# A graph layer on one core: reordering stores, loads, POOL sums and copies around two node loops

## The chip, the cores and the metric

The kernel runs on one core of one Trainium2 chip. The metric is the device time of one launch in microseconds (us); the time before is the median of three runs. The profile is that of one further execution on the hardware.

The core's engines are named as the profile names them: PE is TensorE (its matmuls; PEld are its weight loads), DVE is VectorE, ACT is ScalarE, POOL is GpSimd, SP is SyncE, which here only issues DMA transfers. "SPq" in the profile is SyncE's queue. Each engine runs its own instructions in the order in which the program lists them.

## The reference, cut to what matters

There are 32 graphs of 512 nodes with 256 features each. For each graph:

```python
h = jnp.maximum(_layernorm(x), 0.0)
# branch 1: two convolutions along the node axis
h1 = relu(bn1(conv1(h)))              # 1 tap
x_conv = relu(bn2(conv2(h1)) + h)     # 17 taps
# branch 2: messages over the graph
s = h @ w_se.T + b_se                 # 3 numbers a node
A = jnp.exp(-dist(s)) * adj           # 512 x 512
msg = relu(h @ w_msg.T + b_msg)
x_nmp = jnp.einsum('bnm,bmd->bnd', A, msg)
# a GRU cell of [x_conv, x_nmp] and h
out = x + gru(concat([x_conv, x_nmp]), h)
```

All arithmetic is in float32.

## The kernel before, in words

The graphs are worked through in two groups of 16 (`GB = 16`, `NG = 2`), and then in 16 pairs. The program is written out by hand: inside `tc.manual_schedule()` each engine's instructions stand in the order in which the Python code emits them.

**First part** (`first_part`, one call for each group). For each graph b: load x (`load_x`), layer norm (`statistics`: DVE bn_stats and bn_aggr, then POOL's power for rstd; `normalise`: on DVE, or on ACT with a DVE-made shift), transpose to features by nodes (`transpose_h`, with a store of h to DRAM, HD), the one-tap convolution (`conv1`), and a Fourier transform of windows of 64 nodes (`windows_to_freq`), which is how the 17-tap convolution is computed: it becomes a product per frequency. `between` and `left` bring other work in between: in group 0 the weights' transform, in group 1 the last four products of group 0 (units 36 to 39, run by `fill`) and the gates' weights.

**Node loop** (`nodes`, one call for each group). It walks over the 16 graphs of the group (`todo`) and at the same time over 40 frequencies ("units"). For a unit u, `product` multiplies the group's spectra by the weights in three products (the third with sums: `prepare` has POOL make `wsum` from the loaded weights and `both` from the spectra), and ACT and DVE combine them into y, which is stored to DRAM (YD). Weights come by `load_unit`, 512 KB each, into three buffers; `multiply(u)` first flushes pending stores, runs the product, prepares unit u + 2 and loads the next weights.

For a graph, `message` makes msg and s; `features`, `factors`, `exponents` make exp(-dist) in four tiles; `turn` transposes the loaded adjacency (`load_adj`, 1 MB in four transfers) on DVE, and `masked` multiplies it in, also on DVE; the aggregation is either `aggregate7`, with seven block products in place of eight and eight sums by POOL ahead of it (`block_sums`, `message_sums`, `affinity_sums`), or the plain `aggregate`. Both write a tile `nmp` (one buffer), which is stored to DRAM (ND) by `save_nmp`. `load_h` brings h back from DRAM, and `by_chunks` copies it on ACT into a tile with the tag `hq` (two buffers), which `message` of the same graph reads later.

One iteration i of the loop thus emits, in this order: the loads of adj for the graph after next and of h for the fourth next; the stores that are pending (y of the last unit, nmp of the graph before); factors of the next graph; the first product; the message of the graph after next; half of the mask of the next graph; the second product; the other half; the aggregation of graph b; the h copy; the block sums of the next graph; the third product, if there is one. Group 0 has 36 units for 16 graphs, so two products in most iterations and three in four of them; group 1 has 40 units for its first 13 graphs, three in nearly all. In group 1 the last two graphs use the plain aggregation, since there the next stage begins to use POOL.

**The pairs** (from line 1164): gates of the GRU by products with combined weights (`inverse`, `gates_rz`, `gate_n`), 16 pairs long, from about 860 us to the end.

**What sets the order around the change.** All transfers of the node loops leave one queue, SyncE's. A transfer that has to wait (a store for the engine that makes its data, a load for the readers of the buffer that it overwrites) holds up all behind it in that queue. Likewise on POOL, `wsum` waits for the weights' transfer and for the product that read the buffer before, and everything behind it waits too. The pools named "first", "sums", "seven", "nodes" share memory one after the other: a tile of a later stage waits for the readers of what lay there before.

Of the kernel before, what the change touches and what calls it, by code (L numbers as in the profile page):

```python
# [11 lines left out]
FP = mybir.dt.float32  # L12
# [3 lines left out]
P = 128  # L16
# [49 lines left out]
def gnn_layer(  # L66
# [16 lines left out]
    B, N, D = x.shape  # L83
# [3 lines left out]
    DC = D // P  # L87
# [28 lines left out]
    def load_x(b, queue=nc.sync):  # L116
        X[b] = pools["ahead" if b == GB else "first"].tile([P, NC, D], FP, tag="x", name=f"x_{b}", bufs=1 if b == GB else 3)
        queue.dma_start(X[b], x[b].rearrange("(c p) d -> p c d", p=P))
# [186 lines left out]
    def transpose_h(b):  # L305
# [9 lines left out]
        nc.sync.dma_start(HD[b], HT[b])  # L315
        del XN[b]

    def conv1(b):
        H1[b] = pools["first"].tile([P, NC, D], FP, tag="h1", name=f"h1_{b}", bufs=2)
        h = N // D  # L320
        for c0 in range(0, NC, h):
            p = bank(f"pc1_{b}_{c0}").rearrange("p (c d) -> p c d", d=D)
            for j in range(h):
                c = c0 + j
                for ic in range(DC):
                    nc.tensor.matmul(p[:, j, :], HT[b][:, ic, c * P : (c + 1) * P], w1[:, ic, :],  # L326
                                     start=(ic == 0), stop=(ic == DC - 1))
            h1 = H1[b][:, c0 : c0 + h, :]
            nc.vector.tensor_add(h1, p, shift1_row[:, None, :].to_broadcast([P, h, D]))
            nc.scalar.activation(h1, h1, AF.Relu)  # L330
        if b % GB < GB - 2:
            del HT[b]
# [90 lines left out]
    def by_chunks(b):  # L423
        HQ[b] = work.tile([P, DC, N], FP, tag="hq", name=f"hq_{b}", bufs=2)
        for ic in range(DC):
            nc.scalar.copy(chunks(HQ[b][:, ic, :]), by_chunk(HT[b][:, ic, :]))
        del HT[b]
# [89 lines left out]

    def aggregate(b, dcs=range(2)):
        if 0 in dcs:
            NMP[b] = work.tile([P, DC, N], FP, tag="nmp", name=f"nmp_{b}", bufs=1)  # L520
        for dc in dcs:
            p = bank(f"pn_{b}_{dc}")
            for mc in range(NC):
                nc.tensor.matmul(p, MSG[b][:, mc, dc * P : (dc + 1) * P], A[b][:, mc, :],
                                 start=(mc == 0), stop=(mc == NC - 1))
            nc.scalar.copy(NMP[b][:, dc, :], p)
        if DC - 1 in dcs:
            del MSG[b], A[b]
# [353 lines left out]
    def first_part(g, freq, between, left=()):  # L882


        b0, b1 = g * GB, (g + 1) * GB
        for b in range(b0, b0 + 3):
            if b not in X and (g == 0 or b == b0):
                load_x(b)
        if g == 0:
            t = XN[b0] = pools["first"].tile([P, NC, D], FP, tag="xn", name="rows", bufs=2)  # L890
            ones, diags = t[:, 0, :P], t[:, 1:3, :].rearrange("p i (c m) -> p i c m", m=P)
            nc.vector.memset(ones, 1.0)

            for _ in range(5):
                nc.tensor.matmul(row1[1][:, : 2 * P], ident, fr.rearrange("p c g k -> p (c g k)")[:, : 2 * P], start=True, stop=True)
            batch_norm("bn1", scale1, shift1, nc.gpsimd)
            bn1_row(0, scale1, ones, diags)
            bn1_row(1, shift1, ones, diags)
        if b0 not in STATS:
            statistics(b0)  # L900
        normalise(b0)
        if g == 0:
            scale_w1()
            shift_w1()
        left = list(left)

        def fill():
            for step in left.pop(0) if left else ():
                step()

        if g > 0:
            load_x(b0 + 1)
            fill()
            load_x(b0 + 2)
        transpose_h(b0)
        fill()
        statistics(b0 + 1)
        if g > 0:
            statistics(b0 + 2)
        normalise(b0 + 1, g > 0)  # L920
        fill()
        for b in range(b0, b1):
            if b + 3 < b1:
                load_x(b + 3, nc.sync if b < 3 else nc.gpsimd)
            if b == b0:
                conv1(b)
                one, two = between(0) if g == 0 else ([], [])
                for step in one:
                    step()
                fill()  # L930
                if g == 0:
                    transpose_h(b + 1)
                    statistics(b + 2)
                    normalise(b + 2)
                else:
                    normalise(b + 2)
                    transpose_h(b + 1)
                fill()
                xf, last_two = freq(g), two
                continue  # L940
            if g == 0:

                slots = last_two if b == b0 + 1 else between(b - b0)

                def slot():
                    for step in slots.pop(0) if slots else ():
                        step()

                if b == b0 + 1:
                    between(b - b0)  # L950
                    conv1(b)
                    slot()
                if b == b0 + 2:
                    slot()
                if b == b1 - 1:
                    by_chunks(b - 1)
                    load_h(b0)
                if b + 2 < b1:
                    statistics(b + 2)
                if b + 1 < b1:  # L960
                    transpose_h(b + 1)
                if b > b0 + 2:
                    slot()
                if b + 2 < b1:
                    normalise(b + 2)
                if b > b0 + 1:
                    conv1(b)
                    slot()
                if b == b1 - 1:
                    by_chunks(b)  # L970
                windows_to_freq(b - 1, xf)
                slot()
                continue
            if b + 2 < b1:
                statistics(b + 2)
            if b + 1 < b1:
                transpose_h(b + 1)
            if b + 2 < b1:
                normalise(b + 2)
            one, two = between(b - b0)  # L980
            conv1(b)
            if b == b1 - 1:
                by_chunks(b - 1)
                load_h(b0)
            for step in one:
                step()
            windows_to_freq(b - 1, xf)
            for step in two:
                step()
        if g > 0:  # L990
            by_chunks(b1 - 1)
        windows_to_freq(b1 - 1, xf)
        return xf
# [8 lines left out]
    with tc.tile_pool(name="freq", bufs=1) as fpool:  # L1002
# [33 lines left out]
        def nodes(g, xf, units, last, following=()):  # L1036
# [45 lines left out]
            for i, b in enumerate(todo):  # L1082
                mine = spread(units, i, last) if i < last else []
                more = todo[i + 1 : i + 5]
                seven = i <= last

                def bring():
                    if len(more) > 1:
                        message(more[1])
                        features(more[1])  # L1090

                if g + 1 < NG and i == GB // 2:
                    load_x(b1)
                if g + 1 < NG and i == 3 * GB // 4:
                    statistics(b1)
                if len(more) > 1:
                    load_adj(more[1], i % 2)
                if len(more) > 3:
                    load_h(more[3])
                flush()  # L1100
                if more:
                    factors(more[0])
                if i == 0:
                    bring()
                for u in mine[:1]:
                    multiply(u)
                if i > 0:
                    bring()
                if not seven:
                    aggregate(b, [0])  # L1110
                if more:
                    turn(more[0], [0, 1])
                    exponents(more[0])
                    masked(more[0], [0, 1])
                for u in mine[1:2]:
                    multiply(u)
                if more:
                    turn(more[0], [2, 3])
                    masked(more[0], [2, 3])
                if seven:  # L1120
                    aggregate7(b)
                else:
                    aggregate(b, [1])
                if len(more) > 2:
                    by_chunks(more[2])
                stores.append(partial(save_nmp, b))
                if more and i + 1 <= last:
                    block_sums(more[0])
                for u in mine[2:]:
                    multiply(u)  # L1130
            flush()

        with phase("pw", "ahead"):
# [103 lines left out]
```

## Time and profile before

| what | us |
|---|---|
| median of three runs | 1827.38 |
| lowest, highest | 1824.57, 1829.56 |
| span of the profiled execution | 1824.8 |
| first part, group 0 | 0 to about 152 |
| node loop, group 0 | about 152 to 445 |
| first part, group 1 | about 445 to 565 |
| node loop, group 1 | about 565 to 860 |
| gates of the 16 pairs | about 860 to 1825 |

The stages are read off the timeline by the lines that run. The profile has several views. The page gives busy time by engine and the chain of work that ended last: followed back from the last instruction, each step names what released it. The view of waits lists, for an engine and a line, how long it stood idle and whose instruction ended the wait, as total, number of times and longest. The view of stretches gives busy time in windows. The timeline lists instructions with start, length, engine, source line, output and inputs, and in brackets how long the engine was idle before it, and because of whom. Matmuls are pipelined, and their ends in the profile are modelled, so a stall of TensorE is best measured from start to start.

### The profile page before, as it was taken

The numbers are of one execution on the slowest core, as the hardware profiler recorded it, in microseconds if no ns is written. First come the engines' busy times: TensorE is split into PE (matmuls) and PEld (weight loads), VectorE is DVE, ScalarE is ACT, GpSimd is POOL, SyncE is SP. The second block draws the span as 40 slices with busy tenths as digits, with TensorE's granted clock in tenths as the row PEclk, the third lists the DMA queues.
The fourth block names the chain that finished last, engine by engine and source line by source line (L and its number), as shares of the span: only waits on it lengthen the run. The fifth ranks groups of instructions, "written<-read, shape, count | busy, mean of one in ns | idle before, by whom it ended". The sixth has DMA issues, their size and how long they took to land.

```text
span 1824.8 us, 21188 instructions
## 1 busy us (share of the span) xinstructions
PE 1796.3 (98%) x6974; PEld 1152.3 (63%) x6974; DVE 1244.0 (68%) x2370; ACT 623.0 (34%) x1252; POOL 779.1 (43%) x731
## 2 busy tenths in 40 slices
PE   9999999999999999999999999999999999999998
PEld 6777788788897887886545554555445554555444
DVE  7886889896995787686266556664666456655666
ACT  4556444442345444443212221222222221222121
POOL 3432868777333777776421332223231323133221
PEclk9999999999999999999999999999999999999999
DMA  9999977975668887888242244214422443234412
GB/s 259 310 292 227 248 215 209 240 216 180 232 222 214 232 239 211 228 226 282 68 118 69 56 121 121 87 35 121 121 89 36 118 121 104 50 89 121 116 22 53
DMA packets 307089, 288.27 MB, mean 158 GB/s; under 512 B 146764, under 2 KB 237420, under 8 KB 306596
## 3 DMA queue, kind: packets, MB, share of 16 engines
q1 hardware_dynamic: 296948, 261.44, 53.3%
q0 software_dynamic: 6592, 23.50, 4.1%
q10 hardware_dynamic: 3440, 1.97, 0.4%
q8 instruction: 56, 0.92, 0.2%
q14 instruction: 53, 0.43, 0.1%
HBM read 190.45 MB, written 96.40 MB: 157 GB/s over the span
## 4 chain that ended last, share of the span: by engine, by line
PE 84%; DMA 5%; DVE 4%; POOL 2%; issue 2%; SPq 1%; ACT 1%; ACTq 0%; DVEq 0%; POOLq 0%
PE pg L667 30%; PE pn L667 15%; PE py L390 8%; PE pn L541 8%; PE pc L326 5%; PE pc L655 5%; PE pm L441 4%; PE px L341 3%; DMA wt<-wd 2%; PE pw L254 2%; PE phT L310 1%; PE pd L485 1%; DMA nd<-nmp 1%; PE pz L667 1%; DVE A L491 1%
## 5 line engine op out<-in xcount | busy, mean ns | idle before, releaser
L645 POOL TENSOR_TENSOR hp<-hp 128x512 f32<-128x512 f32 x64 | 80.4, 1267 | 413.9 <-DMA hp<-hd 294.6
L667 PE MATMUL pg<-hp,sw 128*128 128x512 f32 x434 | 222.0, 593 | 0.7 <-DVE rz L686 0.5
L667 PE MATMUL pg<-cp,sw 128*128 128x512 f32 x434 | 221.8, 593 | 0.0
L667 PE MATMUL pg<-np,sw 128*128 128x512 f32 x434 | 221.7, 592 | 0.0
L645 POOL TENSOR_TENSOR cp<-cp 128x512 f32<-128x512 f32 x64 | 80.5, 1267 | 231.8 <-ACT cp L661 230.5
L390 PE MATMUL py<-wt,xf 128*128 128x256 f32 x640 | 156.3, 388 | 0.2 <-DVE y L398 0.2
L682 ACT ACTIVATE rz<-rz,brz 128x512 f32<-128x512 f32 x93 | 67.0, 722 | 260.2 <-DVE rz L686 260.2
L357 POOL TENSOR_TENSOR wsum<-wt 128x512 f32<-128x512 f32 x78 | 102.9, 1319 | 111.0 <-DMA wt<-wd 90.4
L667 PEld LDWEIGHTS pg<-hp,sw 128*128 128x128 f32 x434 | 82.3, 190 | 104.6 <-issue 96.7
L667 PEld LDWEIGHTS pg<-np,sw 128*128 128x128 f32 x434 | 82.6, 190 | 103.7 <-issue 103.7
L667 PEld LDWEIGHTS pg<-cp,sw 128*128 128x128 f32 x434 | 82.6, 190 | 103.7 <-issue 103.7
L390 PEld LDWEIGHTS py<-wt,xf 128*128 128x128 f32 x640 | 118.2, 192 | 35.5 <-issue 20.5
L806 ACT ACTIVATE nt<-nt,vech 128x512 f32<-128x512 f32 x64 | 46.2, 722 | 236.2 <-DVE nt L805 236.2
L441 PE MATMUL pm<-wmsg,hq 128*128 128x259 f32 x512 | 118.5, 383 | 1.0 <-DVE nmp L559 1.0
L326 PE MATMUL pc<-w,hT 128*128 128x256 f32 x512 | 117.9, 383 | 0.8 <-DVE hT L314 0.8
L491 DVE TENSOR_TENSOR A<-A,at 128x512 f32<-128x512 f32 x128 | 113.6, 925 | 6.0 <-ACT A L487 6.0
L667 PE MATMUL pn<-np,sw 128*128 128x512 f32 x224 | 114.5, 593 | 0.0
L667 PE MATMUL pn<-hp,sw 128*128 128x512 f32 x224 | 114.5, 593 | 0.0
L667 PE MATMUL pn<-cp,sw 128*128 128x512 f32 x224 | 114.5, 593 | 0.0
L326 PEld LDWEIGHTS pc<-w,hT 128*128 128x128 f32 x512 | 94.8, 190 | 23.9 <-issue 5.6
L441 PEld LDWEIGHTS pm<-wmsg,hq 128*128 128x128 f32 x512 | 96.2, 190 | 17.2 <-DVE nmp L559 2.5
L655 PEld LDWEIGHTS pc<-back,yt 128*128 128x128 f32 x640 | 92.7, 190 | 7.6 <-issue 7.6
(173 smaller groups left out, 3429.1 us busy)
## 6 DMA issues: line engine op xcount, KB each, us to landing
wt<-wd SPq DMA_DIRECT2D x80, 512.0 KB, 6.9
adj<-in_adj_dram SPq DMA_DIRECT2D x128, 256.0 KB, 7.6
wd<-wst SPq DMA_DIRECT2D x64, 320.0 KB, 5.9
yd<-y SPq DMA_DIRECT2D x76, 256.0 KB, 7.5
yt<-yd SPq DMA_DIRECT2D x30, 640.0 KB, 6.7
hd<-hT SPq DMA_DIRECT2D x32, 512.0 KB, 5.3
nd<-nmp SPq DMA_DIRECT2D x32, 512.0 KB, 4.2
xb<-in_x_dram SPq DMA_DIRECT2D x128, 128.0 KB, 3.7
```

The costliest lines, as they stand in the source:

```text
L326: nc.tensor.matmul(p[:, j, :], HT[b][:, ic, c * P : (c + 1) * P], w1[:, ic, :], start=(ic == 0), stop=(ic == DC - 1))
L341: nc.tensor.matmul(p[:, j * 2 * L : (j + 1) * 2 * L], H1[b][:, c0 + j, ic * P : (ic + 1) * P], fwd, start=True, stop=True)
L357: nc.gpsimd.tensor_tensor(t, WT[g, u][:, 0], WT[g, u][:, 1], op=ALU.add)
L390: nc.tensor.matmul(dst, v[:, ic, :], w[:, ic, :], start=(ic == 0), stop=(ic == DC - 1))
L441: nc.tensor.matmul(p[:, : D + NS], hq[:, ic, c * P : (c + 1) * P], wmsg[:, ic, :], start=(ic == 0), stop=(ic == DC - 1))
L491: nc.vector.tensor_mul(A[b][:, mc, :], A[b][:, mc, :], AT.pop((b, mc)))
L541: nc.tensor.matmul(bk, left[:, k, :], right[:, k, :], start=(first and k == 0), stop=(k == 1), skip_group_check=True)
L645: nc.gpsimd.tensor_tensor(t[:, dst, :], t[:, a, :], t[:, b, :], op=sub)
L655: nc.tensor.matmul(bk[:, t0:t1], YT[p][j][:, c, oc * P : (oc + 1) * P], back[:, n : n + t1 - t0], start=(c == 0), stop=(c == len(spans) - ...
L667: nc.tensor.matmul(bk[:, t], sw[:, k, q, o, :], terms[k][q][:, t], start=(first and i == 0), stop=(i == len(ks) - 1), skip_group_check=True)
L682: nc.scalar.activation(rz[:, g, j, :], src, AF.Sigmoid, bias=brz[:, g : g + 1], scale=1.0)
L806: nc.scalar.activation(n, n, AF.Tanh, bias=b_in[:, i : i + 1], scale=1.0)
```

## The change

The change has six edits, in three functions:

- `nodes`: the pending stores are issued ahead of the loads of adj and h, not behind them, so that a finished nmp or y tile doesn't stand behind loads that wait for their buffers.
- `nodes`: the third product of an iteration, and with it POOL's preparation of the unit after next, stands ahead of POOL's block sums for the next graph.
- `aggregate`: the plain aggregation writes into a tile with the tag hq, of which there are two buffers, in place of nmp, of which there is one.
- `first_part`, group 1: the h copy of the last graph but one, and the load of h that waits for its buffer, stand ahead of the last graph's `conv1` on ACT and SyncE.
- `first_part`, group 1: the statistics of the third graph stand behind the second graph's normalise and a product.
- `conv1` and `first_part`: in group 1 the first h1 tile is placed before the x tiles, under a tag for even and odd graphs with one buffer each in place of one tag with two buffers, so that other tiles share memory with what the node loop used last.

TensorE's instructions and their order stay the same, and no transfer or arithmetic is added or taken away.

```diff
+    def place_h1(b):
+        H1[b] = pools["first"].tile([P, NC, D], FP, tag=f"h1{b % 2}", name=f"h1_{b}", bufs=1)
+
     def conv1(b):
-        H1[b] = pools["first"].tile([P, NC, D], FP, tag="h1", name=f"h1_{b}", bufs=2)
+        if b not in H1:
+            place_h1(b)
...
     def aggregate(b, dcs=range(2)):
         if 0 in dcs:
-            NMP[b] = work.tile([P, DC, N], FP, tag="nmp", name=f"nmp_{b}", bufs=1)
+            NMP[b] = work.tile([P, DC, N], FP, tag="hq", name=f"nmp_{b}", bufs=2)
...
         if g > 0:
+            place_h1(b0)
             load_x(b0 + 1)
             fill()
             load_x(b0 + 2)
         transpose_h(b0)
         fill()
         statistics(b0 + 1)
+        normalise(b0 + 1, g > 0)
+        fill()
         if g > 0:
             statistics(b0 + 2)
-        normalise(b0 + 1, g > 0)
-        fill()
...
+            if b == b1 - 1:
+                by_chunks(b - 1)
+                load_h(b0)
             if b + 2 < b1:
                 statistics(b + 2)
...
             one, two = between(b - b0)
             conv1(b)
-            if b == b1 - 1:
-                by_chunks(b - 1)
-                load_h(b0)
...
+                flush()
                 if g + 1 < NG and i == GB // 2:
                     load_x(b1)
...
                     load_adj(more[1], i % 2)
                 if len(more) > 3:
                     load_h(more[3])
-                flush()
                 if more:
                     factors(more[0])
...
                 stores.append(partial(save_nmp, b))
+                for u in mine[2:]:
+                    multiply(u)
                 if more and i + 1 <= last:
                     block_sums(more[0])
-                for u in mine[2:]:
-                    multiply(u)
```

## The prediction, made before the changed kernel ran

> **What bounds the kernel now.** I read the page first, then five stretches of the span, then what TensorE waited for, then what the SyncE queue waited for, and last the moments around each TensorE stall.
>
> The first two lines are from the page: busy time by engine, and the chain of work that ended last.
>
> ```profile
> PE 1796.3 (98%) x6974; PEld 1152.3 (63%) x6974; DVE 1244.0 (68%) x2370; ACT 623.0 (34%) x1252; POOL 779.1 (43%) x731
> PE 84%; DMA 5%; DVE 4%; POOL 2%; issue 2%; SPq 1%; ACT 1%; ACTq 0%; DVEq 0%; POOLq 0%
> ```
>
> TensorE is the bound nearly everywhere, and its work is not changed by the edit, so the edit can win no more than TensorE's idle time, 1824.8 - 1796.3 = 28.5 us. The stretches (start:end, length, then busy time of PE, PEld, DVE, ACT, POOL, clock, DMA share, GB/s) tell where it lies:
>
> ```profile
> 152.00:445.00 293.00, 286.83 (x1388) 234.53 (x1389) 245.85 (x502) 137.03 (x322) 216.14 (x203) 0.99 0.83 217
> 445.00:565.00 120.00, 118.65 (x693) 107.84 (x693) 95.99 (x272) 51.41 (x123) 44.20 (x47) 1.00 0.67 225
> 565.00:845.00 280.00, 275.19 (x1323) 224.37 (x1321) 213.64 (x469) 128.10 (x301) 197.87 (x197) 0.99 0.87 225
> 845.00:860.00 15.00, 11.75 (x29) 4.95 (x30) 6.22 (x6) 3.39 (x7) 11.92 (x11) 1.00 1.02 405
> ```
>
> They are the node loop of group 0, the first part of group 1, the node loop of group 1, and its tail: 6.2 + 1.4 + 4.8 + 3.3 = 15.7 us idle. The other 12.8 us lie before 152 and after 860, in code that the edit doesn't touch. What ended TensorE's waits (total us, times, longest):
>
> ```profile
> PE pn L524 <- DVE A L491: 3.3, 3, 1.8
> PE py L390 <- POOL both L370: 3.2, 3, 2.0
> PE pn L541 <- ACT nmp L550: 3.0, 2, 1.7
> PE pd L485 <- DVE msg L444: 1.7, 1, 1.7
> PE pn L541 <- POOL ts L516: 1.2, 1, 1.2
> PE phT L310 <- DVE xn L302: 1.1, 1, 1.1
> ```
>
> And how four of them came about, from the timeline (start, length, engine, line; the wait before it in brackets):
>
> ```profile
> 190.55 0.38 SPq L564 DMA_DIRECT2D nd<-nmp  x1
> 198.73 0.37 ACT L548 COPY nmp<-pn 128x256 f32<-128x256 f32 x1 [4.99 <-DMA nd<-nmp]
> 449.49 1.27 POOL L357 TENSOR_TENSOR wsum<-wt 128x512 f32<-128x512 f32 x1 [4.80 <-DMA wt<-wd]
> 450.95 1.41 DVE L283 BATCH_NORM_STATS2 stats<-x 128x6 f32<-128x256 f32 x4 [2.48 <-DMA x<-in_x_dram]
> 558.67 0.33 SPq L414 DMA_DIRECT2D hT<-hd  x1
> 572.75 1.30 DVE L474 STREAM_TRANSPOSE at<-adj 128x512 f32<-128x512 f32 x2 [3.32 <-DMA adj<-in_adj_dram]
> 720.51 1.13 PE L390 MATMUL py<-wsum,both 128*128 128x256 f32 x4 [2.01 <-POOL both L370]
> 847.58 0.58 ACT L526 COPY nmp<-pn 128x512 f32<-128x512 f32 x1 [6.49 <-DMA nd<-nmp]
> ```
>
> A wait row starts at the modelled end of the matmul before. From start to start, less the pace of 216 ns that 12 products in 2.59 us show, the four stalls cost a little more: ACT nmp 1.42 + 1.86 = 3.3 us, POOL both 0.74 + 0.73 + 2.18 = 3.65 us, DVE msg 1.8 us, DVE A 3.75 us. Together 12.5 us.
>
> [...]the SyncE queue stands still for 117.7 us in 22 waits of the nmp store on DVE (5.4 us each), and everything behind it waits too. [...]the same 128x12 copy at L454 takes 0.158 to 1.317 us. So moving POOL work also moves DVE delays; I give that no time of its own.
>
> **The change part by part.**
>
> 1. Stores ahead of loads (flush moved above load_adj and load_h). No instruction is added. In ten iterations of group 0 the nmp store now goes ahead of four adj transfers and one h transfer; elsewhere only a y store moves. Gain: the nmp tile has one buffer, and the ACT copy into it waits for the store to land. The store of 190.55 had its data when DVE L561 ended at 184.7; it stood behind adj (181.78) and h (187.15). Six us earlier it lands before 194, and the 4.99 us wait is gone; likewise the one at 339. Gain 3.3 us. Cost: adj and h now wait for DVE, and the wt load behind them too. At 224.40 the store was issued, at 224.83 the wt load; now adj (1.93) and h (1.24) come between, so wt goes out 3.5 us later. Its reader, POOL wsum, started at 231.47 after waiting for it; with nd, adj, h, yd and wt (2.9 MB) in the queue at 261 GB/s (217 GB/s at 0.83 busy) it lands about 11 to 13 us after 224.4, at 236 or 237. Is that too late? POOL's block sums stand behind it, and the aggregation stalls if they start later than 4.3 us before it (the sixth sum ends 6.0 us after the first begins, as at 710.08 to 716.05, and is read 1.7 us into the aggregation). The next aggregation after the one of 229.97 starts at 249.11, so the sums must start by 244.8 and wsum (1.27) with both (0.73) by 242.8: hidden, by about 6 us. For an iteration of 17 us it is 3 to 4 us, and the transfers of such an iteration (3.7 MB) need 14 of its 17 us. That is narrow, so I take off 1.0 us (bounds: 0, and 2 us in each of ten iterations). Net +2.3.
>
> 2. Third product ahead of block sums. Only POOL's order changes: wsum and both of the next-but-one product (1.27 + 0.73 = 2.0 us) go in front of eight block sums (7.9 us). At 718.00 wsum stood behind sums that ran from 710.08, and TensorE waited until 720.51. Now both ends near 712.2 and the product at 718.3 finds it ready. The sums begin 2.0 us later, at 712.2; their limit is 719.3 - 4.3 = 715. They also wait now for the third product to end on TensorE (the wsum buffer) and for one more wt; in the iteration from 621.84 the product ends at 630.6, the sums start at 633.0 instead of 630.93, against a limit of 636.8 (641.1, the next aggregation without its stall, less 4.3). Gain 3.65; I take 3.6.
>
> 3. h copy ahead of the last conv1. SyncE waited 8.0 us for this copy at L414, with adj of the first node behind it. On ACT the copy can run at 553.7, when the px copies end, instead of 557.52. So load_h goes out at 554.9 instead of 558.67, and adj 3.8 us earlier; the transpose starts at 569.3, when DVE is free, not at 572.75. The message additions behind it release TensorE in time. The relu at 555.33 waits for its own DVE addition until 555.3, so the copy costs nothing. Gain 1.8; I take 1.7.
>
> 4. Plain aggregations into the hq tag. For the last two nodes hq's two buffers have long been read (by the messages of the two iterations before), so ACT L526 at 847.58 doesn't wait for the store of 840.44, and runs when its product ends at 843.9. The exponentials behind it go from 848.06 to 844.6, and the masks end near 851.2 (four at 1.25 and two transposes, slowed by POOL as now) rather than 854.9. TensorE's second node can start at 848.4; only its last block waits, 0.2 us. The gates behind need np sums (ready 857.3), hidden. Gain 3.75; I take 3.4.
>
> 5. statistics(b0 + 2) behind the fill, and h1 placed first. Aim: shift of b0+1 no longer waits on DVE behind the x load of b0+2. But shift also needs rstd from POOL, which stands behind wsum at 449.49 and both, and ends at 452.42; shift ran at 452.75. So it gains 0.3 us. In exchange the statistics (1.9 us) now stand behind the product's y additions, which wait for ACT until 455.3: they run from 456.0 to 457.9 instead of ending at 452.85. Behind them on DVE are the conv1 additions (456.25, now 457.9) and the normalise of b0+2 (459.44, now 461.1); on POOL rstd, and behind it wsum and both of the last leftover product (ended 457.6, then 461). TensorE transposed that normalise's output at 460.00; now 461.7. Cost 1.6 us (bounds: 0, if wt lands 3 us earlier, and 3). The placement moves two memory waits of the loads to work that ended by 441, before these loads leave the queue: nothing.
>
> Sum: 2.3 + 3.6 + 1.7 + 3.4 - 1.6 = 9.4 us. 1827.4 - 9.4 = **1818.0 us**.
>
> **The rivals.**
> - *Everything pays.* The early stores also let wt at 187.39 come sooner (POOL waited 8.06 us for it; two stalls of 0.66 + 1.39 us follow), and part 5 costs nothing: 12.5 + 2.05 = 14.5, so 1812.9. Against it: that wt left the queue at 178.88, ahead of what moves.
> - *Waits change hands.* DVE is 84% busy in group 0's node loop (245.85 of 293) and POOL 74%; the freed time goes to pm waits on DVE nmp L559 (three of 0.5 us now), and the block sums become the new wait. Only the tail and the boundary pay: 1.7 + 3.4 - 1.6 = 3.5, so 1824.
> - *Slower.* SyncE idles behind the store, the DMA engines drain, and wt comes late in each of the ten iterations: each loses 1.7 us, 17 in all, less 2, 3, 4 (8.7) and the 3.3 of part 1, plus 1.6: 1827.4 + 17 - 12.0 + 1.6 = 1834. For it: 0.83 of DMA busy and 5.4 us per store wait. Against it: 3 us or more of slack in every iteration that I worked out.
>
> **How the numbers follow.** Forecast 0.50, everything pays 0.20, waits change hands 0.18, slower 0.12. 0.3% is 5.5 us, so faster means under 1821.9: most of the first, all of the second, little of the third, 0.72; same 0.16; slower 0.12. The range reaches from a little under the second case to just over the third, 1811 to 1827, and leaves out the slower one.
>
> **What would show it.** ACT L548 and L526 without waits on the nd store (part 1, 4); no wait of py on POOL both, and none of pn on POOL ts in its place (2); the first transpose of group 1's nodes near 569 on the old clock (3); phT L310 waiting on DVE xn by 1.5 us more (5). Wrong: longer POOL waits on wt with pn waiting on ts or A in group 0.

## The result, and the profile after

The changed kernel took 1816.49 us (median of four runs, 1813.94 to 1818.6) against 1828.2 us for the kernel before beside it: ratio 0.9938, interval 0.9917 to 0.9960. Timed twice more, beside other kernels, it gave 0.9964 (0.9949 to 0.9978) and 0.9944 (0.9925 to 0.9962). Times the time before of each set, that is 11.3, 6.6 and 10.2 us, 9.4 in the mean. The forecast was 9.4 us. That the mean meets it is luck: three sets that range from 6.6 to 11.3 us don't fix a tenth, and of the five terms of the forecast not all had the right size, so that errors cancelled.

In the views, py is the accumulator of a frequency product, pn that of an aggregation, phT that of a transpose; xn is the normalised x; A is exp(-dist), masked or not, and at the transposed adjacency; POOL's block sums write ts and ms; nd, yd, hd and wd are DRAM copies of nmp, y, h and the transformed weights.

The page of the profile after, busy time by engine and the chain that ended last:

```profile
PE 1791.6 (99%) x6974; PEld 1151.6 (63%) x6974; DVE 1244.6 (69%) x2370; ACT 623.5 (34%) x1252; POOL 779.4 (43%) x731
PE 90%; DMA 3%; DVE 3%; issue 2%; POOL 1%; SPq 0%; ACT 0%; ACTq 0%; DVEq 0%; POOLq 0%
```

TensorE's share of the chain went from 84 to 90%, the share of DMA from 5 to 3%. Its busy time fell by 4.7 us with the same 6974 matmuls: part of what was won is not idle time at all (see the stores and the h copy below). The stretches (start:end, length, busy time of PE, PEld, DVE, ACT, POOL, clock, DMA share, GB/s):

```profile
152.00:437.00 285.00, 283.57 (x1396) 233.43 (x1393) 245.18 (x503) 137.65 (x322) 216.08 (x203) 1.00 0.85 225
437.00:560.00 123.00, 119.02 (x698) 109.89 (x697) 98.58 (x277) 52.08 (x123) 44.34 (x48) 0.99 0.68 225
560.00:816.00 256.00, 256.00 (x1250) 212.12 (x1249) 203.23 (x435) 121.65 (x287) 189.22 (x185) 1.00 0.86 225
...
831.00:846.00 15.00, 7.96 (x17) 2.97 (x14) 6.79 (x8) 2.65 (x5) 12.36 (x11) 0.80 1.03 402
```

Node loop of group 0: 1.4 us idle in place of 6.2. Most of group 1's loop: none. But the first part of group 1 has 4.0 us idle in place of 1.4, at its boundary to the loop before, and the tail has 7.0 us idle in 15. TensorE's waits name these two, and they are new (the third line was there before as well, with 1.2 us):

```profile
PE pn L528 <- DVE A L495: 7.0, 1, 7.0
PE py L394 <- POOL both L374: 4.0, 1, 4.0
...
PE pn L545 <- POOL ts L520: 1.1, 1, 1.1
```

The moments that answer to those shown of before, from the timeline:

```profile
194.88 0.37 ACT L552 COPY nmp<-pn 128x256 f32<-128x256 f32 x1 [0.54 <-PE pn L545]
...
449.64 1.01 POOL L289 TENSOR_TENSOR rstd<-rstd,minus_half 128x4 f32<-128x4 f32 x1 [5.50 <-DVE rstd L288]
...
451.45 1.28 POOL L361 TENSOR_TENSOR wsum<-wt 128x512 f32<-128x512 f32 x1
...
453.46 1.21 PE L394 MATMUL py<-wsum,both 128*128 128x256 f32 x4 [3.98 <-POOL both L374]
...
549.28 0.33 SPq L418 DMA_DIRECT2D hT<-hd  x1
...
563.61 1.30 DVE L478 STREAM_TRANSPOSE at<-adj 128x512 f32<-128x512 f32 x2
...
706.48 1.03 PE L394 MATMUL py<-wsum,both 128*128 128x256 f32 x4
...
838.96 1.30 DVE L478 STREAM_TRANSPOSE at<-adj 128x512 f32<-128x512 f32 x2 [12.48 <-DMA adj<-in_adj_dram]
```

ACT's copy into nmp no longer waits for a store. The product that waited 2.01 us at 720.51 has no wait at 706.48. At the boundary wsum stands behind a power (rstd) that waited 5.5 us for VectorE, and TensorE waits for what comes after it. The first transpose of group 1's nodes, at 563.61, waits for no adj. In the tail VectorE waits 12.5 us for the last adj.

Since the order of TensorE's matmuls is the same in all these kernels, the start of one and the same matmul can be compared: the one at 720.51 before is at 706.48 after, so 14.03 us were won up to there. The table gives how that difference changes over stretches of the old clock (minus is won), each from one profiled execution.

| stretch, old clock | after | again | third time | stores only | third product only | h copy only | hq only | statistics only |
|---|---|---|---|---|---|---|---|---|
| 154-431 loop, group 0 | -9.1 | -6.7 | -7.3 | -6.2 | -1.0 | -3.0 | -4.1 | -0.3 |
| 431-462 boundary | +3.2 | +6.8 | +4.6 | +0.2 | +0.3 | +0.6 | +0.6 | +3.5 |
| 462-575 first part | -0.8 | -0.5 | -0.4 | -0.7 | -0.6 | -1.0 | -0.6 | -0.6 |
| 575-597 first nodes | -4.4 | -4.4 | -4.4 | -0.4 | -0.6 | -4.4 | -0.1 | +2.0 |
| 597-745 loop, group 1 | -4.0 | -4.0 | -3.7 | -3.3 | -4.0 | -1.5 | +0.1 | +1.2 |
| 745-828 its end | 0.0 | 0.0 | 0.0 | +3.9 | 0.0 | 0.0 | 0.0 | 0.0 |
| 828-860 tail | +6.1 | -1.5 | -1.5 | +0.6 | -0.2 | -1.5 | -1.5 | +2.5 |

The third product alone changes little in group 0, and the three columns to its right nothing there, yet those three differ by 0.3 to 4.1 us from the profile of before: that is how far two executions of the same code lie apart in that loop. The rows 462 to 828 repeat to some tenths where the code is the same, save for half clock behind a stall; the boundary and the tail don't always, and are taken up below. So small steps are judged by the timed ratios, and the table tells where.

### The profile page after: what moved, and what is told of

The parts are those of the page before. It is cut to its first block, busy times and chain, and to the rows that moved or that the text cites. A ratio compares the mean times of both kernels' runs of the same rounds, so it can differ in the third digit from the quotient of the medians.

```text
span 1816.8 us, 21203 instructions
## 1 busy us (share of the span) xinstructions
PE 1791.6 (99%) x6974; PEld 1151.6 (63%) x6974; DVE 1244.6 (69%) x2370; ACT 623.5 (34%) x1252; POOL 779.4 (43%) x731
## 4 chain that ended last, share of the span: by engine, by line
PE 90%; DMA 3%; DVE 3%; issue 2%; POOL 1%; SPq 0%; ACT 0%; ACTq 0%; DVEq 0%; POOLq 0%
PE pg L671 30%; PE pn L671 15%; PE py L394 11%; PE pn L545 9%; PE pm L445 6%; PE pc L330 5%; PE pc L659 5%; PE px L345 3%; PE pd L489 2%; PE pw L254 2%; PE phT L310 1%; DMA adj<-in_adj_dram 1%; DMA wt<-wd 1%; PE pz L671 1%; DMA x<-in_x_dram 1%
```

## The experiments

**Each part alone, on the kernel before.** Stores ahead of loads:

```diff
+                flush()
                 if g + 1 < NG and i == GB // 2:
...
-                flush()
```

> The kernel before with the stores ahead of the loads alone. Theory (the early stores both pay and harm): in group 0's node loop TensorE gains about 6 us against before (the two waits of the nmp copies, 3.3 us; the pm stalls, 1.0; the stall at 416, 1.4), and in group 1 the last adj transfers, now behind a y store of 256 KB, land some 10 us later, as in the changed kernel, where VectorE waited 12.5 us for them: 5 to 7 us are lost there again. Sum: 0 to -2 us, ratio 0.999 to 1.000. Rival (the late adj comes from the hq tag or from the third product's place): no such wait here, ratio about 0.997.

Measured 0.9989 (0.9976 to 1.0002): 2.0 us, between -0.4 and 4.4. The gain in group 0's loop is there (-6.2, where unchanged code gave -0.3 to -4.1), and ScalarE's copies no longer wait there for the nd store. The stall of TensorE at 417 in the profile of before, 0.75 us by starts and with half clock right behind it (mean clock 0.66 from 418 to 423), is gone too: it is in all five profiles without this edit (with half clock behind it in three) and in none of the eight with it. The late adj is not there: VectorE waited 3.0 us at most for adj in this profile. What was lost was elsewhere, once in group 0 and once at the end of group 1's loop:

```profile
306.88 1.39 POOL L357 TENSOR_TENSOR wsum<-wt 128x512 f32<-128x512 f32 x1 [5.57 <-DMA wt<-wd]
...
319.23 1.13 PE L390 MATMUL py<-wsum,both 128*128 128x256 f32 x4 [1.21 <-POOL both L370]
...
741.88 1.27 POOL L357 TENSOR_TENSOR wsum<-wt 128x512 f32<-128x512 f32 x1 [7.89 <-DMA wt<-wd]
...
753.75 1.98 PE L390 MATMUL py<-wsum,both 128*128 128x256 f32 x4 [1.97 <-POOL both L370]
```

The second time a wsum waited 7.9 us for its weights (3.9 before), the block sums behind it started at 743.8 and held the next product's wsum until 751.7; TensorE waited 2.0 us and then ran 3.4 us at half clock. The first time it is the same chain with 5.6 us in front, and TensorE waited 1.2 us. Late weights are the price that the prediction feared for this edit. In the profiles with the third product ahead of the sums as well, neither of these two stalls occurs, but late weights make another (see the changed kernel, again).

Third product ahead of block sums:

```diff
+                for u in mine[2:]:
+                    multiply(u)
                 if more and i + 1 <= last:
                     block_sums(more[0])
-                for u in mine[2:]:
-                    multiply(u)
```

> The kernel before with the third product ahead of the block sums alone. Theory: the three waits of py on POOL both in group 1 (3.65 us by starts) go, nothing else changes: -3.6 us, ratio 0.998. Rival (the late adj comes from here, since POOL ends its sums later and the loads move): VectorE waits 10 us or more for the last adj, and the gain is eaten, ratio 1.000 or above.

Measured 0.9978 (0.9969 to 0.9987), 4.0 us. The three waits of py on POOL both are gone, each at its matmul (0.74, 0.73 and 2.17 us by starts). No late adj.

The h copy and the load of h ahead of the last conv1:

```diff
+            if b == b1 - 1:
+                by_chunks(b - 1)
+                load_h(b0)
             if b + 2 < b1:
                 statistics(b + 2)
...
             conv1(b)
-            if b == b1 - 1:
-                by_chunks(b - 1)
-                load_h(b0)
```

> The kernel before with the h copy and the load of h ahead of the last conv1 alone. Theory (the stretch of half clock of 3.4 us at 579.8 in the kernel before is a consequence of the stall just before it, so it goes with the stall): the messages of the first nodes of group 1 come in time, TensorE's 2.7 us around 576 go and 1.7 us of half clock behind them: -4.4 us from start to start over that stretch, ratio 0.9976. Rival (the half clock comes at its own times, whatever TensorE did before): -2.7 us, with a half-clock stretch of 3.4 us still within 10 us of it, ratio 0.9985.

Measured 0.9963 (0.9949 to 0.9976): 6.8 us, the largest of the five. Over 575 to 597 it is 4.4 us, as the first theory has it, and the half clock is gone. From the stretches (the last three columns are clock, DMA share and GB/s), the kernel before, then this one:

```profile
577.00:584.00 7.00, 5.84 (x17) 4.25 (x18) 7.00 (x19) 4.41 (x10) 6.07 (x5) 0.76 1.16 195
```

```profile
574.00:581.00 7.00, 7.00 (x35) 5.88 (x32) 7.00 (x13) 4.83 (x13) 4.51 (x4) 1.00 1.18 202
```

Before, 3.4 of the 7 us were at half clock ((3.6 + 1.7) / 7 = 0.76); here none. This stretch was counted as busy (from 580 to 583, 3.00 us busy of 3.00 at clock 0.50), so no wait shows its 1.7 us. And the rest of the loop ran ahead: TensorE's waits for POOL at the third product fell to 1.4 us in sum (3.2 before), worth 1.5 us, and the nd store ahead of the plain aggregation landed sooner (ScalarE at L526 waited 3.1 us, not 6.5), worth 1.5 in the tail. These two overlap with the third product and with hq, so the parts don't simply add.

Plain aggregations in the hq tag:

```diff
-            NMP[b] = work.tile([P, DC, N], FP, tag="nmp", name=f"nmp_{b}", bufs=1)
+            NMP[b] = work.tile([P, DC, N], FP, tag="hq", name=f"nmp_{b}", bufs=2)
```

> The kernel before with the plain aggregations in the hq tag alone. Theory: ScalarE's copy at L526 no longer waits 6.5 us for the nd store; with adj in time as in the kernel before, TensorE's stalls of 2.0 + 1.0 + 0.7 us in the tail shrink to under 0.5: -3.4 us, ratio 0.998. Rival (the late adj comes with this tile): VectorE waits some 10 us for adj and the tail is 3 to 5 us longer, ratio 1.002.

Measured 1.0003 (0.9990 to 1.0016): no gain that the timing can tell; the trace shows 1.5 us in the tail. The timeline there:

```profile
839.98 0.59 ACT L526 COPY nmp<-pn 128x512 f32<-128x512 f32 x1 [2.85 <-PE pn L524]
...
841.41 5.84 POOL L645 TENSOR_TENSOR hp<-hp 128x512 f32<-128x512 f32 x4 [1.32 <-DMA hp<-hd]
841.72 3.18 DVE L491 TENSOR_TENSOR A<-A,at 128x512 f32<-128x512 f32 x2 [2.80 <-ACT A L487]
...
846.04 3.43 DVE L491 TENSOR_TENSOR A<-A,at 128x512 f32<-128x512 f32 x2
```

ScalarE does not wait for the store any more (it waits for its product). But VectorE's masks, sooner now, meet POOL's four sums for the first pair, and two mask pairs take 3.18 and 3.43 us where they took 2.30 and 2.78 before and take 1.25 where POOL has no sum running.

Statistics behind the product, and the placement of h1 (whose lines are those of the whole change, and are left out here):

```diff
-        if g > 0:
-            statistics(b0 + 2)
         normalise(b0 + 1, g > 0)
         fill()
+        if g > 0:
+            statistics(b0 + 2)
```

> The kernel before with the statistics of the third graph behind the product, and with the h1 tile placed first, alone. Theory (the new stall of 4.1 us at the boundary of the changed kernel comes from this order: POOL's power for that graph waits for VectorE, and the wsum of the last leftover product stands behind it): TensorE waits 3 to 4 us for POOL both there, and the 1.25 us wait of phT on xn goes: +2 to +3 us, ratio 1.001 to 1.0015. Rival (the stall comes only from weights or x that arrive in another order once the stores go first): no wait of py on POOL both at the boundary, phT within 0.5 us of before, ratio 1.000.

Measured 1.0017 (1.0008 to 1.0026): 3.1 us lost. At the boundary:

```profile
455.66 1.40 DVE L283 BATCH_NORM_STATS2 stats<-x 128x6 f32<-128x256 f32 x4
...
457.62 1.01 POOL L289 TENSOR_TENSOR rstd<-rstd,minus_half 128x4 f32<-128x4 f32 x1 [5.51 <-DVE rstd L288]
...
459.44 1.27 POOL L361 TENSOR_TENSOR wsum<-wt 128x512 f32<-128x512 f32 x1
...
461.44 1.57 PE L394 MATMUL py<-wsum,both 128*128 128x256 f32 x4 [3.98 <-POOL both L374]
```

The statistics run late, behind the y additions; POOL's power waits for them, the wsum and both of the last leftover product wait behind the power, and TensorE waits for both. The stall by starts (from the start of one matmul to that of the next, less the usual pace) is 4.15 us, in this kernel and in all three profiles of the whole change alike. The placement of h1 was not run without the statistics, so this run can't tell the two apart; a run further down does, for the stall.

**The changed kernel, again.**

> The changed kernel once more, to learn whether its tail is the same in each execution. Theory (the late adj belongs to the order of its transfers): the profile shows the wait of VectorE for the last adj again, 8 us or more, and of TensorE for it, 4 us or more, and the ratio stays at 0.993 to 0.995. Rival (chance of one execution): under 3 us of both, and the ratio is still in that band, since the stall was not in most of the executions.

> The changed kernel a third time, with more executions. Theory (the 7.0 us wait for the last adj in the first profile was chance, as the second profile had none): under 3 us of TensorE waiting for it, and a ratio of 0.9950 (0.994 to 0.996), between those of the two sets of runs so far. Rival (it belongs to the kernel and comes in about every second execution): 4 us or more again.

The rival of the first and the theory of the second: TensorE waited 2.1 us in sum for the masks of the tail in both. The 7.0 us of the first profile did not come again in these two, nor in the one below with the same order in the tail (the statistics put back). The ratio of the first of these two sets, 0.9964, lies above the band that both sides had given (0.993 to 0.995). Issue to landing of the adj transfers that left after 799 us (min, median, max), first profile (four transfers), then the second (eight):

```profile
DMA to landing us min/median/max: 5.1/13.8/19.8
```

```profile
DMA to landing us min/median/max: 4.6/6.1/8.4
```

In the first, between 822 and 838, POOL's queue (q0) had 78.5% of the DMA engines' time and SyncE's (q1) 24.9%. Why adj came late in one execution and not in two others, whose order is the same, is left open.

Both profiles have a wait that the first lacks, at the last aggregation of group 0. It is on POOL's block sums; from the third profile:

```profile
408.09 1.34 POOL L361 TENSOR_TENSOR wsum<-wt 128x512 f32<-128x512 f32 x1 [5.44 <-DMA wt<-wd]
...
428.74 1.13 PE L545 MATMUL pn<-A,msg 128*128 128x256 f32 x4 [0.36 <-POOL A L520]
...
430.65 1.13 PE L545 MATMUL pn<-ts,ms 128*128 128x256 f32 x4 [0.78 <-POOL ts L520]
```

By starts this is 1.4 to 1.8 us, in six of the seven profiles of the changed kernel and its versions, and in none of the six others. In each of the six a wsum waited 5.3 to 6.2 us for its weights some 20 us earlier, and POOL had no pause from there on; in the seventh, the first profile, no wsum waited for weights there. Over group 0's loop (152 to 440) POOL's wsum waited 44 to 55 us for weights in the eight profiles with the stores first, and 27 to 38 us in the five without. So late weights come with the first edit in the whole change too, and cost TensorE something there.

**Put back, and carried on.** Four edits on the changed kernel. The last adj ahead of the y store:

```diff
+                ahead = g > 0 and more[1:] == todo[-1:]
+                if ahead:
+                    load_adj(more[1], i % 2)
                 flush()
```

> The changed kernel with the last graph's adj transfers put back ahead of the pending y store (only for that graph; all other stores stay ahead). Theory (adj lands late because a y store of 256 KB and 1 us of waiting for VectorE go ahead of it, and what is left of it then shares the DMA engines with POOL's transfers for the first pair, which took 0.3 MB of 0.38 MB per us): VectorE's wait for adj falls from 12.5 to about 1 us and TensorE's 7.0 us to under 1.5: 5 to 6 us faster than the changed kernel, ratio 0.990 to 0.991. Rival (the crowding by POOL's transfers happens in any order, or the wait was chance): the same ratio as the changed kernel within 0.001.

Measured 0.9952 (0.9934 to 0.9970) beside 0.9964 for the changed kernel in the same set: no difference to be told, so the rival rather than the theory. The tail is that of the second profile.

The statistics back ahead of the normalise:

```diff
+        if g > 0:
+            statistics(b0 + 2)
         normalise(b0 + 1, g > 0)
         fill()
-        if g > 0:
-            statistics(b0 + 2)
```

> The changed kernel with the statistics of the third graph put back ahead of the second graph's normalise, as before. Theory (this order alone makes the 4.1 us stall at the boundary, as it made 4.15 us in the kernel before with this part alone): the wait of py on POOL both at about 453 goes, phT waits for xn about 1 us as before: 3 us faster than the changed kernel, ratio 0.992. Rival (with the other edits x of the third graph is there sooner or later than in the kernel before, so VectorE now waits for it and shift, xn and phT are late): as fast as the changed kernel or slower.

Measured 0.9932 (0.9909 to 0.9956), beside 0.9964. The wait of py on POOL both at the boundary is gone, phT waits 1.1 us for xn there, as before:

```profile
PE phT L310 <- DVE xn L302: 1.8, 2, 1.1
```

The placement of h1 stayed. So the order of the statistics makes the stall, and the change is better without it. What the placement is worth (the forecast: nothing) was not measured alone.

Against both stalls at once: the last adj ahead as above, and POOL's preparation of the last product moved up, rather than the statistics back:

```diff
-                        [partial(product, pw, 0, u1, xf), partial(load_unit, 0, u3)],
-                        [partial(prepare, pw, 0, u3, xf), partial(product, pw, 0, u2, xf)],
+                        [partial(product, pw, 0, u1, xf), partial(load_unit, 0, u3), partial(prepare, pw, 0, u3, xf)],
+                        [partial(product, pw, 0, u2, xf)],
```

> The changed kernel with the last adj ahead of the y store, and with wsum and both of the last leftover product put on POOL right behind the product before the last but one, so ahead of the power that they waited for. Theory: both new stalls go, 7.0 + 4.1 us less what else then ends the wait (1.5 in the tail, 1 at the boundary): 8 us faster than the changed kernel, ratio 0.989. Rival (the tail was chance, only the boundary pays): ratio 0.992.

Measured 0.9925 (0.9902 to 0.9948), median 1811.25 us: the rival's number. The product doesn't wait; phT does, 2.5 us for xn, and 3.4 us of half clock follow. The next edit is on top of this one:

```diff
-                        [partial(prepare, pw, 0, u1, xf), partial(product, pw, 0, u0, xf), partial(prepare, pw, 0, u2, xf)],
+                        [partial(prepare, pw, 0, u1, xf), partial(product, pw, 0, u0, xf)],
+                        [partial(prepare, pw, 0, u2, xf)],
...
         statistics(b0 + 1)
+        fill()
         normalise(b0 + 1, g > 0)
```

> The changed kernel with the last adj ahead of the y store, wsum and both of the last leftover product right behind the product before the last but one, and now also the second graph's power on POOL ahead of wsum and both of the last product but one. Theory (at the boundary, phT still waited 2.5 us for xn in the version without this, since that power stood behind wsum and both, so ScalarE's normalise, its y copies, and VectorE's chain behind them were late): the power ends 2 us sooner, phT waits under 0.7 us, and the half clock that followed goes: 3 us faster than that version, ratio 0.991. Rival (VectorE or the x load becomes what xn waits for): phT still waits 2 us, ratio 0.9925.

Measured 0.9926 (0.9912 to 0.9941), median 1812.62: no better, as the rival had it. The power now comes 3.4 us before the next product (448.07) where it came 1.35 us before, but half of that is lost at once:

```profile
445.68 1.27 POOL L361 TENSOR_TENSOR wsum<-wt 128x512 f32<-128x512 f32 x1
445.74 1.22 DVE L296 SCALAR_TENSOR_TENSOR shift<-mv,rstd 128x4 f32<-128x4 f32 x1 [1.14 <-POOL rstd L289]
```

The shift of 4 numbers a partition, 0.16 us elsewhere, takes 1.22 us while wsum runs on POOL, and phT still waits 1.7 us. Both versions are ahead of the kernel before by about 13.5 us and of the changed kernel by some 4 us in the mean of its sets. Beside the changed kernel in the same set, the interval of the first ends just below where the changed kernel's begins (0.9948 and 0.9949); that of the second overlaps with it.

## Why the prediction was right in sum, and where it was not

| step | forecast, us | alone, timed, us | verdict |
|---|---|---|---|
| 1 stores first | -2.3 | -2.0 (-4.4 to +0.4) | fits; the interval includes no gain |
| 2 third product first | -3.6 | -4.0 (-5.7 to -2.4) | right |
| 3 h copy first | -1.7 | -6.8 (-9.3 to -4.4) | a fourth of it |
| 4 hq tag | -3.4 | +0.5 (-1.8 to +2.9) | not shown; 1.5 in the trace |
| 5 statistics, h1 | +1.6 | +3.1 (+1.5 to +4.7) | half of it |
| sum | -9.4 | -9.2 | |

The sum of the parts alone, -9.2, is close to the whole by chance too: in the traces the stores alone lost 3.9 us at the end of group 1's loop that the whole change does not lose, and about 3 us of the h copy's gain are won by the third product or by hq as well. And the limit that the prediction set, TensorE's 28.5 us of idle time, left out that TensorE's busy time can shrink too: it shrank by 4.7 us. Two stretches of half clock in the profile of before, 3.4 us each at 419 and 580 and counted as busy, are gone from it; two others came, 3.4 us at 454 and 6.8 us at 840, so how much of the 4.7 us is half clock was not shown.

1. The gain had its cause: in every profile with this edit ScalarE no longer waited in group 0's loop for the nd store, and TensorE not for ScalarE's nmp. Of the 3.3 us only the stall at 199 is sure, in all five profiles without the edit and in none with it; the one of 1.86 us at 340 was gone in the profile of hq alone too, whose code there is that of before. The stall at 417 and its half clock were won besides, and not forecast. The cost of 1.0 us had its cause as well: POOL waited longer for weights in group 0, and TensorE lost 1.4 us to it with the edit alone and 1.4 to 1.8 us in most profiles of the whole change. But of the ten iterations that were feared it is one each time. The loss in group 1 (the 3.9 us of the table), which the prediction did not look for, came with the edit alone and not in the whole change.
2. Right, wait by wait. No wait on the block sums took their place in group 1; the one in group 0 comes with the late weights of step 1.
3. The mechanism held: the h load left the queue at 549.28, and the start of the first transpose, 563.61, is 569.4 on the old clock (5.76 us were won up to the matmul at 575.1), where 569.3 was forecast. The term that was mis-sized is "Gain 1.8": it counted one stall of TensorE. From start to start 2.7 us went, and 1.7 us of half clock right behind them, which the prediction left out, and everything later in the loop stood better.
4. ScalarE's copy ran at 843.9 on the old clock, as forecast (839.98, and 3.96 us that this run was ahead). The failed step is "the masks end near 851.2 (four at 1.25 and two transposes, slowed by POOL as now)": the masks ended at 853.4, from 854.9, since POOL's sums slowed them by more than now. And where the h copy is early, the tail is 1.5 us shorter without hq, and no shorter with both: what hq adds to the whole change is not shown.
5. The failed step is "Cost 1.6 us", which took the wait of phT as the whole cost. The same sentence had wsum and both of the last product end at 461 in place of 457.6, and TensorE needed them at 457.89: those 3.1 us were not charged. They were the stall, 4.15 us as measured; phT's own wait of 1.25 us went in exchange. The half clock behind the stall (mean clock 0.66 from 454 to 459 after) was left out here as well.

Of the rivals, "everything pays" (1812.9 of 1827.4, a ratio of 0.9921) lies inside the interval of the first set and outside those of the two others, and its reason fails: step 5 cost twice the forecast. "Waits change hands" did happen, in three places, and cost about 6 us (4.15 - 1.25 at the boundary, 3.4 - 1.5 between masks and POOL's sums in the tail, and in two of the three profiles 1.4 on the block sums in group 0), not the whole gain. "Slower" needed weights late enough to stop TensorE in ten iterations of group 0; the profiles of the changed kernel show at most one.

## What to carry to other kernels

Where an instruction is moved back on one engine, follow what then waits on the next engine's queue down to the last reader, and charge each late reader on the path, not just the one that the edit was made for. A stall's price here was its length and, where the clock fell behind it, that too (2.7 and 1.7 us at 576): read the clock column of the microseconds after a stall, since half clock was counted as busy. And measure the parts alone, and some together: a sum that comes out right says little of its terms, and gains that overlap don't add.

## What the runs showed of the hardware

- Half clock after stalls. The trace's clock fell to one half (0.50) for 3.4 or 6.8 us at a time (the last microseconds of a run apart): from 579.8 to 583.2 before, for one. With the late h copy (five profiles) such a stretch came within 5 us of the stall of TensorE at 576 each time; with the early one (eight profiles) never. The 4.15 us stall at the boundary had one within 2 us of its end in all five profiles that had the stall, the stalls of 2.7 and 1.9 us in its place in the two last versions as well, the 1.25 us of the others in none of six. But it is no rule of the stall's length alone: 2.2 us at the third product had none behind them in the profiles of before and of hq alone, and one in that of the statistics alone; the same 1.4 us in the tail had one in one of six profiles; and once, at 175 in the third profile, one came with no wait over 0.2 us before it in that loop. What decides is left open.
- VectorE beside POOL's sums. The shift of 4 numbers a partition took 0.16 us before, and 1.22 us in the last version, where it began 0.06 us after a 128x512 addition on POOL. In the tail a pair of masks took 1.25 us with no sum on POOL, and beside POOL's sums 2.30 and 2.78 us before and 3.18 and 3.43 us with hq alone. Of the 32 copies of 128x12 at L454 before, 18 took 0.76 to 1.32 us: each began within 0.01 us of a sum on POOL and ended 0.02 to 0.04 us after the sum did. The other 14 took 0.16 to 0.43 us, and four of these began with a sum too.
- In the first profile of the changed kernel TensorE waited 7.0 us for the last adj's masks, in the second 2.1 us in sum for the masks of the tail, and neither the order, which is the same, nor the other executions explain the difference.
